# Mamba decays from one product, order of the first chunks and of the square sums, the span of layer 1's GLU, and routing scratch in a weight slot: a four-layer model on one Trainium2 core

## The chip, the core and the metric

The program runs on one NeuronCore of a Trainium2 chip. A time is the device time of one execution in microseconds (us). Before the change three runs gave 3191.99, 3198.89 and 3201.08 us, with a median of 3198.89. One further execution was taken by the hardware profiler, and the times of single instructions below come from it.

## The reference

The input x has 4 sequences of 512 tokens with 256 features, in fp32. Four layers follow, each of the same form:

```
xn = layernorm(x)
x  = x + attention(xn) + ffn(xn)
```

Only the first three matter for the change.

- Layer 0: the attention is a Mamba2 mixer with 32 heads of 64 features and a state of 128. A projection gives a gate, the stream x_s, B, C and a step dt. The state obeys `h = dA_t * h + dt_t * x_t B_t`, with `dA = exp(-dt * exp(A_log))`, and the output is `y_t = h C_t + D x_t`. It is multiplied by silu(gate), scaled by the inverse root of its mean square over all 2048 features, and projected to 256. The feed-forward part is a GLU, `(silu(x Wg) * (x Wu)) Wd`, with 1024 hidden features.
- Layer 1: latent attention with 16 heads of 192 query features and 128 value features, and as feed-forward part a GLU as above plus product-key experts: each token gathers 8 of 512 rows from two tables.
- Layer 2: a mixing of heads within a token, and 8 experts of which each token takes two, plus one shared GLU. Layer 3 is full attention plus experts chosen by a probability mass, and no part of the change touches its work.

## The kernel before, in words

**Tiles.** Tokens are cut into 16 tiles of 128 (`NTILE`), four (`TPB`) per sequence, and 4 sequences (`NB`). Weights are pre-arranged on the host into "units", and `Ctx.unit` (DMA at L53) loads one into a slot "wu" of [128, 3072] fp32. From layer 1 on there are three such slots, in turn: a load waits until the last reader of the unit that had the slot before is through. [...]

**What sets the order.** Every part of a layer is a Python generator that emits instructions and yields an estimate of their TensorE time. `weave` always advances the stream with the smallest ratio of what it has yielded to the total that the call gives for it (with a start offset). A scheduler then orders instructions on each engine by what was emitted and what is ready, except those marked `keep_in_program_order`, and puts in the semaphores. [...] SyncE (SP) issues most DMAs.

**Layer 0** (`mamba_pieces`, woven at L649 with the GLU). The mixer is computed in chunks of 128 tokens for groups of 8 heads: 16 pairs i of sequence and group, four chunks t each.

- `time_steps` computes log dA for all tokens into `dA` [128 tokens, 16 tiles, 32 heads]. Per sequence, four transposes (L326) turn it to [32 heads, 128 tokens], and four products with the triangle `c.le` (L327) give its running sums over a chunk. ScalarE takes the exponential of each (L333), VectorE sets the first column of the one to zero, and two DMAs on SP store them in DRAM as `own` and `since`. L342 makes two more sums over the tokens.
- `decays` (L405) reads `own` back, spread over 128 partitions, as G. `products` (L415) runs a VectorE scan over G, which gives the decay between any two tokens of the chunk. `before` makes the tokens-major x_s (transposes L429, xdt L431), scales x_s by D (L435), and reads `since` as eb.
- `before_gpsimd` multiplies G by C B (L449) and makes xw = xdt times the decay to the chunk's end (L452), both on GpSimd.
- `within` uses them: state times C (L470, then L471 and L472), new state xw times B (L478, L481 to L484), G times xdt (L488), sum and gate (L493, L494), squares (L496).
- `project_out` multiplies y by the output weights into `po` (L510), 256 columns of a "tr" bank. `acc` takes it over (L516; ScalarE's copy for the first group). For the last pair, i = 15, six products with one column of ones (L523) then sum the squares into column 256 of the same bank, and ScalarE copies that column (L527).

Ahead of the loop the first two chunks are prepared by hand, in this order: decays 0 and 1, products 0 and 1, before 0, before_gpsimd 0.

**Layer 1** (`layer1`). Latent attention (16 heads of 4 sequences: scores and softmax L672, L675, L679, L792, their transposes L799 and L803, values and output L935, L941 and L949), the product-key experts (gathers by GpSimd's indirect DMA, L1053) and the GLU (`glu_pieces`: gate and up products L134, activation, down products L212) are woven. The experts' pools and the GLU's pool lie on the right side of SBUF. The stream `room()` starts at 0.915 of the weave: it closes the right side and opens the pools of layer 2 there, loads layer 2's small weights and experts, and runs the routing of the first half of the tokens.

**Layer 2** (`Layer2`). Tokens are taken in two halves. `Half.dispatch` computes router probabilities, ranks and the slots of each token (`router`, L1385, L1447, all small VectorE steps in tiles of the pool "t_route"). `gather` fetches token rows by 23 indirect DMAs (L1482) from `xn_half`, the experts follow (transposes L1500, copies L1505, products L1512 and L1534, results L1539, stores to slots_out L1541), and `combine` gathers the results. The shared GLU's weights are the unit `t_shared`; the units `f_units` are layer 3's attention weights, loaded ahead.

The functions that the diff touches, with their callers:

Of the kernel before, what the change touches and what calls it, by code (L numbers as in the profile page):

```python
# [11 lines left out]
AF = mybir.ActivationFunctionType  # L12
# [3 lines left out]
P = 128  # L16
# [229 lines left out]
def mamba_pieces(c, a, ws, open_pool):  # L246
# [41 lines left out]
    def time_steps():  # L288

        wide_tile = lambda tag: c.tile(pool, wide, tag)  # L290

        pd = c.ps()
        for t in range(NTILE):
            project_tokens(
                c, pd[:, t * 32 : (t + 1) * 32], w_bcd, slice(256, 288),
                slice(t * P, (t + 1) * P),
            )
        z, e = wide_tile("S"), wide_tile("S")
        nc.vector.tensor_add(z, v3(pd, 32), dt_bias[:, None, :].to_broadcast(wide))
        nc.vector.scalar_tensor_tensor(e, z, -1.0, z, ALU.mult, ALU.min)  # L300
        nc.scalar.activation(e, e, AF.Exp)
        expA = c.tile(keep, [P, 32], "expA")
        tc.keep_in_program_order(nc.scalar.activation(expA, a_log, AF.Exp))
        yield 20.0
        s, w, q = wide_tile("xw"), wide_tile("xw"), wide_tile("eb")
        nc.vector.tensor_scalar_add(s, e, 2.0)
        nc.vector.reciprocal(s, s)
        nc.vector.tensor_mul(s, s, e)
        nc.vector.tensor_mul(w, s, s)
        nc.vector.tensor_scalar_mul(q, w, 1.0 / 17.0)  # L310
        yield 20.0
        for k in range(7, 0, -1):
            nc.vector.scalar_tensor_tensor(q, q, 1.0 / (2 * k + 1), w, ALU.add, ALU.mult)
        nc.vector.scalar_tensor_tensor(q, q, 1.0, s, ALU.add, ALU.mult)
        nc.vector.tensor_scalar_max(z, z, 0.0)
        nc.vector.scalar_tensor_tensor(dt, q, 2.0, z, ALU.mult, ALU.add)
        dA = wide_tile("eb")
        nc.vector.scalar_tensor_tensor(
            dA, dt, -1.0, expA[:, None, :].to_broadcast(wide), ALU.mult, ALU.mult
        )  # L320
        yield 38.0
        for b in range(NB):
            pa, pc = c.ps("tr"), c.ps("acc")
            for t in range(TPB):
                cols = slice(t * P, (t + 1) * P)
                nc.tensor.transpose(pa[:32, cols], dA[:, b * TPB + t, :], c.ident)  # L326
                nc.tensor.matmul(  # L327
                    pc[:32, cols], lhsT=dA[:, b * TPB + t, :], rhs=c.le, start=True, stop=True
                )
            tiles = slice(b * TPB, (b + 1) * TPB)  # L330
            for src, out in ((pa, own), (pc, since)):
                row = c.tile(pool, [P, TPB, P], "sq")[:32]
                nc.scalar.activation(row, v3(src[:32, :], P), AF.Exp)  # L333
                if out is own:
                    nc.vector.memset(row[:, :, 0:1], 0.0)
                nc.sync.dma_start(out[tiles].rearrange("t h s -> h t s"), row)
            yield 1.5

        dAf = dA.rearrange("p t h -> p (t h)")
        for tri, out in ((c.gt, after), (c.ones, etot)):  # L340
            pc = c.ps()
            nc.tensor.matmul(pc, lhsT=tri, rhs=dAf, start=True, stop=True)  # L342
            nc.scalar.activation(out.rearrange("p t h -> p (t h)"), pc, AF.Exp)
        yield 2.0
# [100 lines left out]
    def before_gpsimd(i, t):  # L445
        b, g = i // 4, i % 4
        chunk = chunks[i, t]
        G, xdt = chunk[:2]
        nc.gpsimd.tensor_mul(G, G, seqs[b][2][:, t, :][:, None, :].to_broadcast([P, HG, P]))  # L449
        if t < TPB - 1:  # L450
            chunk[2] = xw = c.tile(pool, [P, 512], "xw")
            nc.gpsimd.tensor_mul(  # L452
                v3(xw, HD), v3(xdt, HD), by_head(after[:, b * TPB + t, g * HG : (g + 1) * HG])
            )

    state, sums = {}, []

# [46 lines left out]
    def project_out(i, t, y, sq):  # L504
# [4 lines left out]
        for k in range(4):  # L509
            nc.tensor.matmul(  # L510
                po, lhsT=y[:, k, :], rhs=groups[i][1][:, k, :], start=(k == 0), stop=(k == 3)
            )
        if g == 0:
            nc.scalar.copy(acc[:, t, :], po)
        else:
            nc.vector.tensor_add(acc[:, t, :], po, acc[:, t, :])  # L516
        if i == 15:

            if t == 0:
                sums.append(c.tile(pb, [P, TPB], "sums", bufs=1))  # L520
            parts = [ssq[:, t, k, :] for k in range(2)] + [sq[:, k, :] for k in range(4)]
            for k, part in enumerate(parts):
                nc.tensor.matmul(  # L523
                    bank[:, DM : DM + 1], lhsT=part, rhs=c.ones[:, :1], start=(k == 0),
                    stop=(k == 5),
                )
            nc.scalar.copy(sums[0][:, t : t + 1], bank[:, DM : DM + 1])  # L527
        if g == 3 and t == TPB - 1:
            if i == 15:
                pss = sums[0]  # L530
# [27 lines left out]
    decays(0, 0)  # L558
    decays(0, 1)
    products(0)  # L560
    products(1)
    before(0, 0)
    before_gpsimd(0, 0)
    behind = None
    for i in range(16):
        for t in range(TPB):
# [55 lines left out]
def layer0(c, a, x_in, con):  # L622

    with ExitStack() as stack:
# [12 lines left out]
        def glu_units():  # L637
# [8 lines left out]
        c.parts(2, lambda b: layernorm(c, b, c.xn[b * SEQ : (b + 1) * SEQ, :]))  # L646
        weave(
            c,
            (mamba_pieces(c, a, ws, open_pool), 650.0, 0.0),  # L649
            (glu_units(), 207.0, 0.0),  # L650
        )

# [438 lines left out]
def layer1(c, a, xn, following):  # L1091


    with ExitStack() as stack, ExitStack() as right:
        def pool_of(name, bufs, stack=stack, **kw):
            return stack.enter_context(c.tc.tile_pool(name=name, bufs=bufs, **kw))

        p_keep, p_t, glu = (pool_of(name, 1, right, side="right") for name in ("p_keep", "p_t", "g1"))
        dram = pool_of("p_dram", 1, space=bass.MemoryType.DRAM)
        keep = pool_of("l_keep", 1)  # L1100
        latent = latent_pieces(c, a, keep, lambda: pool_of("l_h", 2))
# [6 lines left out]
        def room():  # L1108
# [6 lines left out]
            c,  # L1115
            (latent, 457.0, 0.0),
            (product_key_pieces(c, a, p_keep, p_t, dram, xn), 237.0, 0.02),
            (glu_units(), 145.0, 0.0),
            (room(), 270.0, 0.915),
            flush=False,  # L1120
        )
# [173 lines left out]
    nc.vector.tensor_mul(s, s, m[:, :, None].to_broadcast(wide))  # L1295


def router(c, pool, wr, bs, p=None, wide=1):

    nc = c.nc
# [15 lines left out]
    yield 2.0  # L1318
    full = [P, n, E, E]
    other, own = p[:, :, None, :].to_broadcast(full), p[:, :, :, None].to_broadcast(full)  # L1320
    before = c.tile(pool, full, "before", bufs=wide)
    tie = c.tile(pool, full, "before" if wide > 1 else "tie", bufs=wide)
    nc.vector.tensor_tensor(before, other, own, ALU.is_gt)
    nc.vector.tensor_tensor(tie, other, own, ALU.is_equal)
    low = v3(c.low, E)[:, None, :, :].to_broadcast(full)
# [10 lines left out]
class Half:  # L1336
# [13 lines left out]

    def dispatch(self):
        c, k, pool, nc = self.c, self.k, self.pool, self.c.nc
        tile = lambda shape, tag, **kw: c.tile(pool, shape, tag, **kw)
        p, rank = tile([P, HT, E8], "p_half"), tile([P, HT, E8], "rank")
        before = yield from router(c, pool, k["router"], [2 * self.hf, 2 * self.hf + 1], p, 4)
        yield 2.0
        nc.vector.tensor_reduce(rank, before[2], AX.X, ALU.add)

# [76 lines left out]
        ats = []  # L1435
        four = [P, 4, P]
        for i in range(2 * HT // 4):
            ats.append(tile(four, "before", bufs=4))
            nc.vector.tensor_tensor(
                ats[i], k["iota"][:, None, :].to_broadcast(four),  # L1440
                part[:, 4 * i : 4 * i + 4][:, :, None].to_broadcast(four), ALU.is_equal,
            )
            yield 1.0
# [238 lines left out]
def program(tc, a, x_in, out):  # L1682
    nc = tc.nc
    with ExitStack() as stack:
# [4 lines left out]
        c.ident, c.le, c.gt, c.ones, c.neg, c.dup = (  # L1689
            con[:, k : k + P] for k in (C_ID, C_LE, C_GT, C_ONE, C_NEG, C_DUP)  # L1690
        )
        c.iota, c.low = con[:, C_IOTA : C_IOTA + 64], con[:, C_LOW : C_LOW + 64]
        eps = c.tile(c.keep, [P, 2], "eps")
        nc.vector.memset(eps[:, 0:1], 1e-5)
# [178 lines left out]
```

## Time and profile before

| what | us |
|---|---|
| median of three runs | 3198.89 |
| the profiled execution | 3204.3 |
| its span, first to last instruction | 3202.2 |
| TensorE (PE) busy | 3099.3 |
| VectorE (DVE) busy | 1820.1 |
| ScalarE (ACT) busy | 1257.2 |
| GpSimd (POOL) busy | 637.9 |

The mean clock granted to TensorE was 0.985 of full speed. On the chain of work that ended last, TensorE holds 85% of the span, VectorE 7%, ScalarE 2% and GpSimd 2%.

Times in the views run from the first instruction. Layer 0 lies at 0 to about 818 us, layer 1 to 1541, layer 2 to about 1760, and layer 3 fills the rest with TensorE busy throughout. An fp32 product shows in the trace as two matmul records, a transpose as one. "Idle before it" and the name behind the arrow say how long an engine stood before an instruction and what released it; "issue" or "remote" there means that the profile names no engine for it.

| DMA from SP | issued at, us |
|---|---|
| t_shared, 768 KB | 1322.96 |
| f_units, first, 1536 KB | 1412.91 |
| f_units, second | 1492.64 |
| f_units, third | 1682.11 |

### The profile page before, as it was taken

The numbers are of one execution on the slowest core, as the hardware profiler recorded it, in microseconds if no ns is written. First come the engines' busy times: TensorE is split into PE (matmuls) and PEld (weight loads), VectorE is DVE, ScalarE is ACT, GpSimd is POOL, SyncE is SP. The second block draws the span as 40 slices with busy tenths as digits, with TensorE's granted clock in tenths as the row PEclk, the third lists the DMA queues.
The fourth block names the chain that finished last, engine by engine and source line by source line (L and its number), as shares of the span: only waits on it lengthen the run. The fifth ranks groups of instructions, "written<-read, shape, count | busy, mean of one in ns | idle before, by whom it ended". The sixth has DMA issues, their size and how long they took to land.

```text
span 3202.2 us, 35743 instructions
## 1 busy us (share of the span) xinstructions
PE 3099.3 (97%) x12534; PEld 1898.2 (59%) x12534; DVE 1820.1 (57%) x4644; ACT 1257.2 (39%) x2918; POOL 637.9 (20%) x509
## 2 busy tenths in 40 slices
PE   8999999999999999998788999999999999999999
PEld 5566666666655555555566566665665655555555
DVE  5777877788587777777354654555545522222222
ACT  4544444453566665666223433333333311111111
POOL 0565555556100233320223000000000000000000
PEclk9999999999999999998799999999999999999999
DMA  3333323332311244443223000000000000000000
GB/s 111 98 109 119 105 83 106 119 99 73 101 38 50 72 117 99 120 113 104 56 64 122 11 1 27 1 27 1 21 1 1 20 20 20 20 20 20 0 0 27
DMA packets 89090, 185.12 MB, mean 58 GB/s; under 512 B 14192, under 2 KB 57216, under 8 KB 84176
## 3 DMA queue, kind: packets, MB, share of 16 engines
q1 hardware_dynamic: 74448, 135.05, 13.0%
q0 software_dynamic: 14176, 47.01, 5.8%
q8 instruction: 99, 1.62, 0.2%
q10 hardware_dynamic: 288, 0.79, 0.1%
q14 instruction: 79, 0.65, 0.1%
HBM read 160.92 MB, written 12.98 MB: 54 GB/s over the span
## 4 chain that ended last, share of the span: by engine, by line
PE 85%; DVE 7%; ACT 2%; POOL 2%; another core or an unknown queue 2%; issue 1%; DMA 1%; SPq 0%; ACTq 0%; DVEq 0%; POOLq 0%
PE mm L134 33%; PE acc L212 8%; PE mm L672 8%; PE mm L142 5%; PE acc L1182 4%; PE acc L688 3%; PE tr L510 2%; PE tr L1174 2%; PE tr L799 2%; PE acc L935 2%; PE acc L949 1%; PE acc L488 1%; PE mm L1512 1%; PE tr L212 1%
## 5 line engine op out<-in xcount | busy, mean ns | idle before, releaser
L134 PE MATMUL mm<-xnT,wu 128*128 128x512 f32 x2128 | 956.5, 597 | 1.1 <-DVE cy L280 0.9
L134 PEld LDWEIGHTS mm<-xnT,wu 128*128 128x128 f32 x2128 | 402.5, 192 | 466.8 <-issue 446.0
L679 ACT ACTIVATE pr<-pr,nm 128x128 f32<-128x128 f32 (+3 forms) x512 | 285.6, 558 | 295.4 <-DVE nm L675 256.4
L202 DVE TENSOR_TENSOR hT<-sg,mm 128x512 f32<-128x512 f32 x176 | 120.6, 685 | 401.3 <-PE mm L134 387.9
L201 ACT ACTIVATE sg<-mm 128x512 f32<-128x512 f32 x176 | 104.6, 594 | 585.6 <-PE mm L134 585.1
L675 DVE CUSTOM_DVE_ANT_0 pr<-mm,late 128x128 f32<-128x128 f32 (+3 forms) x512 | 245.6, 483 | 101.5 <-PE mm L672 89.5
L212 PE MATMUL acc<-wu,hT 128*128 128x256 f32 x1280 | 288.6, 381 | 4.4 <-DVE os L1539 4.4
L212 PEld LDWEIGHTS acc<-wu,hT 128*128 128x128 f32 x1280 | 242.3, 191 | 53.6 <-issue 17.2
L134 PE MATMUL mm<-xnT,w_in 128*128 128x512 f32 x512 | 229.8, 593 | 0.4 <-DVE cy L280 0.4
L1053 POOL DMA_INDIRECT e<-in_p_experts,ids x128 | 129.5, 1012 | 505.4 <-DVE x L152 364.9
L280 DVE SCALAR_TENSOR_TENSOR cy<-mm,ws,cy 128x509 f32<-128x509 f32 (+2 forms) x216 | 160.5, 745 | 49.7 <-ACT cy L276 45.7
L672 PE MATMUL mm<-kf,qf 128*128 128x128 f32 (+3 forms) x512 | 179.7, 450 | 4.1 <-DVE qf L776 2.8
L672 PE MATMUL mm<-k,q 128*128 128x128 f32 (+3 forms) x512 | 178.1, 438 | 1.0 <-DVE q L1147 1.0
L449 POOL TENSOR_TENSOR G<-G,CB 128x1024 f32<-128x1024 f32 x64 | 153.1, 2393 | 101.2 <-DVE G L415 98.0
L435 ACT ACTIVATE xD<-xc,ws 128x128 f32<-128x128 f32 x256 | 83.9, 391 | 197.2 <-POOL y L472 187.5
L134 PEld LDWEIGHTS mm<-xnT,w_in 128*128 128x128 f32 x512 | 96.5, 190 | 104.7 <-issue 95.8
L152 DVE SCALAR_TENSOR_TENSOR x<-acc,cw,x 128x256 f32<-128x256 f32 x128 | 61.9, 484 | 153.6 <-PE acc L212 153.5
L1182 PE MATMUL acc<-PT,V 128*128 128x512 f32 (+3 forms) x512 | 149.1, 433 | 0.0
L415 DVE TENSOR_TENSOR_SCAN G<-G,eye 128x1024 f32<-128x1024 f32 x64 | 146.9, 2296 | 0.0
L1147 DVE TENSOR_SCALAR q<-mm,bias 128x512 f32<-128x512 f32 x64 | 48.0, 751 | 165.1 <-PE mm L134 165.1
L799 PEld LDWEIGHTS tr<-con,pr 128*128 128x128 f32 x640 | 81.3, 143 | 101.1 <-issue 36.6
L799 PE MATMUL tr<-con,pr 128*128 128x128 f32 x640 | 123.5, 284 | 18.3 <-DVE PT L803 6.8
(346 smaller groups left out, 4949.0 us busy)
## 6 DMA issues: line engine op xcount, KB each, us to landing
G<-own SPq DMA_DIRECT2D x64, 512.0 KB
w_in<-in_m_units SPq DMA_DIRECT2D x16, 1024.0 KB
eb<-since SPq DMA_DIRECT2D x96, 128.0 KB
wu<-in_o_units SPq DMA_DIRECT2D x8, 1536.0 KB
wo<-in_m_units SPq DMA_DIRECT2D x16, 512.0 KB
psw<-pes SPq DMA_DIRECT2D x128, 64.0 KB
wu<-in_g_units SPq DMA_DIRECT2D x4, 1536.0 KB
wu<-in_f_units SPq DMA_DIRECT2D x4, 1536.0 KB
```

What stands on the lines that cost most here:

```text
L134: c.nc.tensor.matmul(out, lhsT=w[:, d, cols], rhs=c.xnT[:, d, tokens], start=(d == 0), stop=(d == 1))
L142: c.nc.tensor.matmul(out, lhsT=c.xnT[:, d, tokens], rhs=w[:, d, cols], start=(d == 0), stop=(d == 1))
L212: nc.tensor.matmul(po[:, j, :], lhsT=hT[k][:, (t + j) * P : (t + j + 1) * P], rhs=wd[:, k, :], start=(i == 0), stop=(i == per - 1),)
L280: nc.vector.scalar_tensor_tensor(y[:, j:], src[:, : SEQ - j], conv[:, k, 3 - j : 4 - j], y[:, j:], ALU.mult, ALU.add,)
L415: tc.keep_in_program_order(nc.vector.tensor_tensor_scan(flat, flat, eye.rearrange("p h t -> p (h t)"), 0.0, ALU.mult, ALU.add))
L449: nc.gpsimd.tensor_mul(G, G, seqs[b][2][:, t, :][:, None, :].to_broadcast([P, HG, P]))
L672: nc.tensor.matmul(sc, lhsT=q[:, i * P : n], rhs=k[:, :n], start=True, stop=True)
L675: nc.vector.tensor_tensor_reduce(out=pr, in0=sc, in1=late[:, SEQ - n :], scale=1.0, scalar=-NEG, op0=ALU.add, op1=ALU.min, accum_out=nm,)
L679: nc.scalar.activation(pr, pr, AF.Exp, bias=nm, scale=-1.0, accum_out=total)
L799: nc.tensor.transpose(pt[:, (i - j) * P : (i - j + 1) * P], prs[s][i][:, j * P : (j + 1) * P], c.ident)
L1053: nc.gpsimd.indirect_dma_start(out=e, out_offset=None, in_=a["p_experts"], in_offset=bass.IndirectOffsetOnAxis(ap=ids[:, t, k : k + 1], ax ...
L1182: nc.tensor.matmul(z[:, j * P :], lhsT=head["V"][:, j, h, :], rhs=head["PT"][:, j, j * P :], start=(j == 0), stop=(j == TPB - 1),)
```

## The change

The change has six parts.

1. The decays of one sequence come from one product. The left operand is `dA` of four tiles, 128 tokens by 4 x 32, and the right operand is `c.ident_le`, the identity and the triangle side by side (columns that already lie next to each other in `con`). The result [4 x 32, 256] holds the turned values and the running sums; one exponential, one memset and the same two DMAs follow. The stream's estimates are lowered to match (0.5 for 1.5, and 646 for 650 in all).
2. In the first pair of chunks, `before_gpsimd`'s operations keep program order, and the scan of chunk 1 is emitted after the GpSimd work of chunk 0. On GpSimd the order becomes G 0, xw 0, G 1, xw 1, where it was G 0, G 1, xw 0, xw 1.
3. In `project_out` the sums of squares are emitted directly after the product `po`, ahead of the addition that reads it.
4. The pool of layer 1's GLU moves to the left side, which `room()` doesn't close, and the stream's total is 126 in place of 145, so that its work is spread over more of the weave.
5. In `router` and `dispatch` the tiles before, tie, sel, cum, pick, hit and ats are no longer tiles of the pool, but parts of one weight slot "wu". With this, the turn of the slots changes: each half's dispatch takes one of the three.
6. `c.ident_le` is defined.

```diff
--- before.py
+++ after.py
@@ -320,21 +320,19 @@
         )
         yield 38.0
         for b in range(NB):
-            pa, pc = c.ps("tr"), c.ps("acc")
-            for t in range(TPB):
-                cols = slice(t * P, (t + 1) * P)
-                nc.tensor.transpose(pa[:32, cols], dA[:, b * TPB + t, :], c.ident)
-                nc.tensor.matmul(
-                    pc[:32, cols], lhsT=dA[:, b * TPB + t, :], rhs=c.le, start=True, stop=True
-                )
+
             tiles = slice(b * TPB, (b + 1) * TPB)
-            for src, out in ((pa, own), (pc, since)):
-                row = c.tile(pool, [P, TPB, P], "sq")[:32]
-                nc.scalar.activation(row, v3(src[:32, :], P), AF.Exp)
-                if out is own:
-                    nc.vector.memset(row[:, :, 0:1], 0.0)
-                nc.sync.dma_start(out[tiles].rearrange("t h s -> h t s"), row)
-            yield 1.5
+            pa = c.ps("tr")[:, : 2 * P]
+            nc.tensor.matmul(
+                pa, lhsT=dA[:, tiles, :].rearrange("p t h -> p (t h)"), rhs=c.ident_le,
+                start=True, stop=True,
+            )
+            rows = c.tile(pool, [P, TPB, P], "sq")[:, :2, :]
+            nc.scalar.activation(rows, v3(pa, P), AF.Exp)
+            nc.vector.memset(rows[:, 0, 0:1], 0.0)
+            for k, out in enumerate((own, since)):
+                nc.sync.dma_start(out[tiles].rearrange("t h s -> (t h) s"), rows[:, k, :])
+            yield 0.5
 
         dAf = dA.rearrange("p t h -> p (t h)")
         for tri, out in ((c.gt, after), (c.ones, etot)):
@@ -446,12 +444,16 @@
         b, g = i // 4, i % 4
         chunk = chunks[i, t]
         G, xdt = chunk[:2]
-        nc.gpsimd.tensor_mul(G, G, seqs[b][2][:, t, :][:, None, :].to_broadcast([P, HG, P]))
+
+        keep_order = tc.keep_in_program_order if i == 0 and t < 2 else lambda ins: ins
+        keep_order(
+            nc.gpsimd.tensor_mul(G, G, seqs[b][2][:, t, :][:, None, :].to_broadcast([P, HG, P]))
+        )
         if t < TPB - 1:
             chunk[2] = xw = c.tile(pool, [P, 512], "xw")
-            nc.gpsimd.tensor_mul(
+            keep_order(nc.gpsimd.tensor_mul(
                 v3(xw, HD), v3(xdt, HD), by_head(after[:, b * TPB + t, g * HG : (g + 1) * HG])
-            )
+            ))
 
     state, sums = {}, []
 
@@ -510,10 +512,6 @@
             nc.tensor.matmul(
                 po, lhsT=y[:, k, :], rhs=groups[i][1][:, k, :], start=(k == 0), stop=(k == 3)
             )
-        if g == 0:
-            nc.scalar.copy(acc[:, t, :], po)
-        else:
-            nc.vector.tensor_add(acc[:, t, :], po, acc[:, t, :])
         if i == 15:
 
             if t == 0:
@@ -525,6 +523,10 @@
                     stop=(k == 5),
                 )
             nc.scalar.copy(sums[0][:, t : t + 1], bank[:, DM : DM + 1])
+        if g == 0:
+            nc.scalar.copy(acc[:, t, :], po)
+        else:
+            nc.vector.tensor_add(acc[:, t, :], po, acc[:, t, :])
         if g == 3 and t == TPB - 1:
             if i == 15:
                 pss = sums[0]
@@ -558,9 +560,9 @@
     decays(0, 0)
     decays(0, 1)
     products(0)
-    products(1)
     before(0, 0)
     before_gpsimd(0, 0)
+    products(1)
     behind = None
     for i in range(16):
         for t in range(TPB):
@@ -646,7 +648,7 @@
         c.parts(2, lambda b: layernorm(c, b, c.xn[b * SEQ : (b + 1) * SEQ, :]))
         weave(
             c,
-            (mamba_pieces(c, a, ws, open_pool), 650.0, 0.0),
+            (mamba_pieces(c, a, ws, open_pool), 646.0, 0.0),
             (glu_units(), 207.0, 0.0),
         )
 
@@ -1095,7 +1097,8 @@
         def pool_of(name, bufs, stack=stack, **kw):
             return stack.enter_context(c.tc.tile_pool(name=name, bufs=bufs, **kw))
 
-        p_keep, p_t, glu = (pool_of(name, 1, right, side="right") for name in ("p_keep", "p_t", "g1"))
+        p_keep, p_t = (pool_of(name, 1, right, side="right") for name in ("p_keep", "p_t"))
+        glu = pool_of("g1", 1)
         dram = pool_of("p_dram", 1, space=bass.MemoryType.DRAM)
         keep = pool_of("l_keep", 1)
         latent = latent_pieces(c, a, keep, lambda: pool_of("l_h", 2))
@@ -1115,7 +1118,7 @@
             c,
             (latent, 457.0, 0.0),
             (product_key_pieces(c, a, p_keep, p_t, dram, xn), 237.0, 0.02),
-            (glu_units(), 145.0, 0.0),
+            (glu_units(), 126.0, 0.0),
             (room(), 270.0, 0.915),
             flush=False,
         )
@@ -1295,8 +1298,7 @@
     nc.vector.tensor_mul(s, s, m[:, :, None].to_broadcast(wide))
 
 
-def router(c, pool, wr, bs, p=None, wide=1):
-
+def router(c, pool, wr, bs, p=None, room=None):
 
 
     nc = c.nc
@@ -1318,8 +1320,12 @@
     yield 2.0
     full = [P, n, E, E]
     other, own = p[:, :, None, :].to_broadcast(full), p[:, :, :, None].to_broadcast(full)
-    before = c.tile(pool, full, "before", bufs=wide)
-    tie = c.tile(pool, full, "before" if wide > 1 else "tie", bufs=wide)
+    if room is None:
+        before, tie = c.tile(pool, full, "before"), c.tile(pool, full, "tie")
+    else:
+        before, tie = (
+            v.rearrange("p (t e f) -> p t e f", e=E, f=E) for v in (room[:, :512], room[:, 512:1024])
+        )
     nc.vector.tensor_tensor(before, other, own, ALU.is_gt)
     nc.vector.tensor_tensor(tie, other, own, ALU.is_equal)
     low = v3(c.low, E)[:, None, :, :].to_broadcast(full)
@@ -1350,9 +1356,22 @@
 
     def dispatch(self):
         c, k, pool, nc = self.c, self.k, self.pool, self.c.nc
-        tile = lambda shape, tag, **kw: c.tile(pool, shape, tag, **kw)
+
+        room = c.tile(c.weights, [P, 3072], "wu")
+        ends_at = [2048]
+
+        def tile(shape, tag):
+            if tag not in ("sel", "cum", "pick", "hit"):
+                return c.tile(pool, shape, tag)
+            n = int(np.prod(shape[1:]))
+            flat = room[:, ends_at[0] : ends_at[0] + n]
+            ends_at[0] += n
+            if len(shape) == 3:
+                return v3(flat, shape[2])
+            return flat.rearrange("p (a b c) -> p a b c", b=shape[2], c=shape[3])
+
         p, rank = tile([P, HT, E8], "p_half"), tile([P, HT, E8], "rank")
-        before = yield from router(c, pool, k["router"], [2 * self.hf, 2 * self.hf + 1], p, 4)
+        before = yield from router(c, pool, k["router"], [2 * self.hf, 2 * self.hf + 1], p, room)
         yield 2.0
         nc.vector.tensor_reduce(rank, before[2], AX.X, ALU.add)
 
@@ -1435,7 +1454,7 @@
         ats = []
         four = [P, 4, P]
         for i in range(2 * HT // 4):
-            ats.append(tile(four, "before", bufs=4))
+            ats.append(v3(room[:, i * 512 : (i + 1) * 512], P))
             nc.vector.tensor_tensor(
                 ats[i], k["iota"][:, None, :].to_broadcast(four),
                 part[:, 4 * i : 4 * i + 4][:, :, None].to_broadcast(four), ALU.is_equal,
@@ -1689,6 +1708,7 @@
         c.ident, c.le, c.gt, c.ones, c.neg, c.dup = (
             con[:, k : k + P] for k in (C_ID, C_LE, C_GT, C_ONE, C_NEG, C_DUP)
         )
+        c.ident_le = con[:, C_ID : C_ID + 2 * P]
         c.iota, c.low = con[:, C_IOTA : C_IOTA + 64], con[:, C_LOW : C_LOW + 64]
         eps = c.tile(c.keep, [P, 2], "eps")
         nc.vector.memset(eps[:, 0:1], 1e-5)
```

## The prediction

> **What bounds the kernel now.** First the page: the busy totals, the slices and the chain.
>
> ```profile
> span 3202.2 us, 35743 instructions
> PE 3099.3 (97%) x12534; PEld 1898.2 (59%) x12534; DVE 1820.1 (57%) x4644; ACT 1257.2 (39%) x2918; POOL 637.9 (20%) x509
> ...
> PE   8999999999999999998788999999999999999999
> ...
> PEclk9999999999999999998799999999999999999999
> ```
>
> TensorE is busy for 3099.3 of 3202.2 us. So a change gains in three ways only: less TensorE work, less of the 102.9 us of idle time, or less time at a reduced clock. The slices put both losses at 1440 to 1760 us. The stage windows, read second, split them (columns: window, then length and busy us of PE, PEld, DVE, ACT and POOL, clock, DMA share, GB/s):
>
> ```profile
> 20.00:240.00 220.00, 219.83 (x949) 131.30 (x950) 150.25 (x194) 102.47 (x201) 92.67 (x57) 1.00 0.27 87
> 240.00:790.00 550.00, 541.22 (x2644) 342.05 (x2643) 430.42 (x562) 247.60 (x514) 316.69 (x203) 1.00 0.32 102
> ```
> ```profile
> 1443.20:1453.40 10.20, 7.05 (x16) 3.94 (x17) 6.19 (x23) 5.80 (x17) 3.25 (x3) 0.50 0.44 121
> 1508.10:1514.90 6.80, 6.23 (x17) 4.18 (x18) 4.31 (x22) 4.97 (x14) 0.00 (x0) 0.50 0.16 53
> 1525.10:1531.90 6.80, 6.80 (x19) 4.33 (x19) 1.87 (x12) 1.24 (x3) 0.00 (x0) 0.50 0.00 0
> 1552.40:1579.70 27.30, 5.91 (x14) 3.89 (x13) 3.63 (x8) 3.79 (x5) 13.39 (x15) 0.50 0.36 73
> ```
>
> Layer 0 is bound by TensorE alone: what is cut there at 70 us reaches 240 with nothing to wait for (0.17 us idle), and only 8.8 us are idle from there to 790. The end of layer 1 (1400 to 1541) and layer 2 (to 1760) are not: there the clock stands at half in pieces. Third, the timelines of the two places in layer 0 that are edited (start, length, engine, line, operation, idle before and its releaser):
>
> ```profile
> 73.04 0.27 PE L326 MATMUL tr<-con,eb 128*32 128x128 f32 x1
> 73.24 0.41 PE L327 MATMUL acc<-con,eb 128*32 128x128 f32 x2
> 73.58 0.28 PE L326 MATMUL tr<-con,eb 128*32 128x128 f32 x1
> ```
> ```profile
> 791.65 1.02 PE L478 MATMUL mm<-xw,Btok 128*128 128x512 f32 x2
> ...
> 792.95 2.28 DVE L415 TENSOR_TENSOR_SCAN G<-G,eye 128x1024 f32<-128x1024 f32 x1
> ...
> 795.15 0.40 DVE L516 TENSOR_TENSOR acc<-tr,acc 128x256 f32<-128x256 f32 x1
> ...
> 795.60 0.61 PE L523 MATMUL tr<-con,ssq 128*128 128x1 f32 x4 [2.93 <-DVE acc L516]
> ```
>
> A transpose and its product take 0.55 us of TensorE (73.04 to 73.58). In the second, TensorE stands 2.93 us for an addition of 0.40 us that is queued behind a scan of 2.28 us.
>
> [...]
>
> **The change, part by part.**
>
> *Decays (L322 to L336).* Removed on TensorE: 8 pairs from 67.69 to 72.08 us (4.39), 4 from 73.04 to 75.23 (2.19), and the last 4 apart, 0.44 for the transposes and 0.95 for the products: 7.97 us. Added: 4 products of 128x256, two records each. In the window 1100 to 1200, 32 records of this shape (L212) take 7.44 us, 0.233 each, so 8 take 1.86. Gain 7.97 - 1.86 = 6.1; if the new product also shows its 0.19 us weight load each time, 5.4, the lower end. ScalarE does 4 exponentials of [128, 256] for 8 of [32, 512]; it is busy 9 of the 20 us there and bounds nothing. The DMAs stay two per sequence at the same place of SP's queue, ahead of the `eb` and G loads, which wait for them as before; the G load issued at about 78 us serves a scan at 93, so 10 us of slack.
>
> *First chunks (L449, L452, L558 to L563).* No work changes. GpSimd now multiplies G 0, xw 0, G 1, xw 1, where it did G 0, G 1 (6.51 us from 95.52), xw 0 at 101.99. TensorE came for xw 0 at 102.9 and waited 0.17 us. By the decays it comes 6 us earlier, about 96.9, and would wait some 6 us; with the new order xw 0 is ready after one G product and the 1.04 us of xw, some 3.3 us sooner and moved up with the scans. Gain 0.2 by itself; it keeps the 6.1. Behind the waiting product on TensorE stand the next chunk's products and the GLU filler; if xw 0 is late, up to 3 us of the 6.1 are lost.
>
> *Sums (L516, L523).* Placed ahead of the reading addition, six one-column products per tile wait only for squares made earlier. The 2.93 us wait goes; the half-clock piece of 798.1 to 801.5, which costs 1.7, may go too. The addition now waits for the sums (0.61 + 1.03 us on TensorE), and VectorE, nearly full at 792 to 801, is late next: its chain to the next output product doesn't shorten. Ends 1 and 4.6; I take 3.
>
> *Layer 1's GLU.* The work is the same, its last sequence comes later. A sequence of one unit is 15.0 us of L134 and 7.4 of L212 (one in each 100 us from 1100 to 1400). Before, the last ended at 1436, where 82% of the L672 score products are placed; after, at 95%. By the order on TensorE 11 to 19 us of GLU move beyond that point. Lost there, 1436 to 1541: about 10.5 us idle, and 23.8 us at half clock, so 11.9. Of this, 4.25 idle (1442 to 1447) falls on every engine at once beside a run of gathers, with no engine named as releaser: no filler helps, nor the half clock that follows it. The 3.9 idle at 1504 to 1509 and the two later half-clock pieces (6.8) come when the GLU is over again. Left: 2.6 idle, some 3 of clock at 1446 to 1453, and what the 1508 piece gives. Against it, 13% thinner filler at 900 to 1400, where 13 us are idle: 1 to 2 more. Also, VectorE gets 7 us of GLU steps where it is 60 to 75% busy. Ends -3 and +14; I take +5.
>
> *Routing scratch in a weight slot.* No operation changes. But slots rotate: by the order on SP, read against times before, the `t_shared` load moves from 1323 to about 1493, still ahead of its use at 1527; `f_units` 0 and 1 (1.5 MB each) move from 1413 and 1493 to about 1546 and 1626, beside the two runs of 23 gathers. On SP the first stands ahead of the first slots_out stores (1597), the second between two stores, behind a routing product that TensorE has already passed. The gathers are issued every 1.25 us and move 92 GB/s at 1541 to 1580; windows elsewhere reach 186 GB/s. With 1.5 MB more in 29 us, 92 + 54 = 146 GB/s, still below; I take 0.5, ends 0 and 10 for both.
>
> Sum: 6.1 + 0.2 + 3 + 5 - 0.5 = 13.8 us. The profiled execution took 3204.3 us (span 3202.2, 2.1 around it), so 3190.5 of its kind; it lay 5.4 above the median 3198.89. Against the median, 3185.1.
>
> **Rivals.**
>
> *Late GLU gives nothing.* For it: the stalls beside gathers stop all engines. Against: 2.6 us of plain waits lie in reach. Then 13.8 - 5 = 8.8 gained; with -1 for thin filler and clock, 3191.
>
> *Late GLU closes the whole tail.* If those stalls are waits that other work can fill: 10.5 + 11.9 = 22.4, less 2 for thin filler and less what lies after 95%, 14 to 16. Then 13.8 + 10 = 24, 3175.
>
> *Slower: loads beside the gathers of layer 2.* TensorE stands for 20.67 us (L1512, releaser ACT xsT) until 1575, when the last gather has landed; a like gap comes at 1638. If a load of 1.5 MB holds the gathers back for its whole time at their rate, 1.57/0.092 = 17 us, twice, 34: 3199 - 14 + 34 = 3219. From 7 us each the gain is gone; from 12 each the kernel is measurably slower. For it: that gap is the longest on TensorE, and its cause is open. Against: DMA share 0.36 there.
>
> *The decays' saving is swallowed* (the chain own, G, scan, G times CB, xw arrives no sooner, or the product is no cheaper): 3191, one with the first rival in its number.
>
> **How the numbers follow.** Forecast 0.45 (3178 to 3192), late GLU or decays without gain 0.28, whole tail 0.14, slower by the loads 0.10, other 0.03. About 0.3% is what a measurement of this kernel can tell from no change: 9.6 us, so below 3189.3 and above 3208.5. Faster: 0.37 of the forecast, 0.11 of the first rival, 0.14 of the third case, 0.62. Slower: 0.08 of the loads and 0.02 of other, 0.10. Same: 0.28. The range leaves out the best of the whole tail and most of the loads: 3168 to 3201.
>
> **What would show it.** In the profile of after: 8 records of the new product at about 0.23 us, and the first L134 after them 6 us sooner; xw's product with no wait over 1 us near 97 us; no wait of L523 on L516; L212 records up to about 1510 and fewer half-clock pieces before 1541; the first gap of layer 2 no longer than 20.7 us. I am wrong if the gathers' gap grows by over 7 us, if PE idle at 900 to 1400 rises by over 5, or if TensorE waits for xw.

## The result and the profile after

| | before | changed |
|---|---|---|
| median of six runs, us | 3197.89 | 3175.51 |
| lowest and highest | 3191.99 to 3204.61 | 3166.72 to 3178.26 |

The ratio is 0.993, with a 95% interval of 0.9915 to 0.9945: 22.4 us faster (18 to 27). The forecast was 13.8. The page of the changed kernel, the same lines as before:

```profile
span 3171.8 us, 35654 instructions
...
PE 3078.8 (97%) x12494; PEld 1883.7 (59%) x12494; DVE 1819.0 (57%) x4644; ACT 1251.1 (39%) x2912; POOL 638.6 (20%) x509
...
PE   8999999999999999999788999999999999999999
...
PEclk9999999999999999999899999999999999999999
```

TensorE's idle time fell from 102.9 to 93.0 us and its busy time by 20.5. Busy time includes what half clock adds: in the trace of before, four L134 records take 3.55 us to the next line's start at 1527.1, where the granted clock is 0.50, and 1.80 at 29.9, where it is 1.00. So half of the time at half clock is counted as lost below, an estimate from these two. The two profiled spans differ by 30.4 us, 8 more than the medians. Of this, 5.6 us lie ahead of every edit: an L134 pair takes 2.06 us until about 26 us in the one execution and until 16 in the other, and 1.10 from there on. So the stages are compared from a fixed record of layer 0's GLU (at 37.0 and 31.3 us) to the first score product of layer 1 (at 878.4 and 849.5): 841.5 us before, 818.2 after. By then the changed kernel is 23.3 us ahead, and from there to the end it gains 1.5 more. But some 3.4 of the 23.3 are not gained, only moved: 8 records of L134, 0.43 us each, stand ahead of that score product before and behind it in the changed kernel, as in all traces with the late GLU. So about 20 us lie in layer 0 and the head of layer 1, and about 5 behind.

The decays, on TensorE's timeline of the changed kernel (mm, tr and acc are tags of the kernel's PSUM pool, with 4, 2 and 2 tiles):

```profile
62.07 1.03 PE L326 MATMUL tr<-con,eb 128*128 128x256 f32 x4
62.94 1.88 PE L340 MATMUL mm<-eb,con 128*128 128x512 f32 x4
64.65 1.03 PE L326 MATMUL tr<-con,eb 128*128 128x256 f32 x4
65.52 2.74 PE L134 MATMUL mm<-xnT,w_in 128*128 128x512 f32 x6
```

From each start to the next line's start four records take 0.87 us (62.07 to 62.94, 64.65 to 65.52): 1.74 us in all, for 7.97 before. The sums, on the timeline at the end of layer 0:

```profile
771.62 1.89 PE L512 MATMUL tr<-wo,y 128*128 128x256 f32 x8
...
773.35 0.50 PE L521 MATMUL tr<-con,ssq 128*128 128x1 f32 x4
...
777.40 0.41 DVE L529 TENSOR_TENSOR acc<-tr,acc 128x256 f32<-128x256 f32 x1
```

They follow their product with no idle time, and the addition comes 4 us behind them, with nobody waiting. Last, layer 1 in two windows, before and after:

```profile
880.00:1408.00 528.00, 513.25 (x2218) 294.30 (x2217) 408.83 (x1412) 334.84 (x897) 106.57 (x105) 0.99 0.32 83
1408.00:1541.00 133.00, 119.47 (x547) 73.00 (x546) 90.09 (x318) 85.65 (x209) 16.04 (x17) 0.91 0.33 105
```
```profile
880.00:1380.00 500.00, 482.13 (x2083) 271.98 (x2083) 383.35 (x1319) 316.83 (x849) 109.20 (x110) 1.00 0.33 83
1380.00:1512.00 132.00, 124.15 (x571) 75.90 (x568) 90.30 (x312) 83.97 (x206) 12.28 (x13) 0.95 0.28 82
```

In the last window TensorE idles 7.9 us for 13.5, and its mean clock is 0.95 for 0.91 (6.6 us lost for 12, if the missing share of the clock is taken as time). In the window ahead of it, it idles 17.9 us for 14.8: the filler is thinner.

### The profile page after: what moved, and what is told of

Read it like the earlier page. It is cut to its first block, busy times and chain, and to the rows that moved or that the text cites. A ratio compares the mean times of both kernels' runs of the same rounds, so it can differ in the third digit from the quotient of the medians.

```text
span 3171.8 us, 35654 instructions
## 1 busy us (share of the span) xinstructions
PE 3078.8 (97%) x12494; PEld 1883.7 (59%) x12494; DVE 1819.0 (57%) x4644; ACT 1251.1 (39%) x2912; POOL 638.6 (20%) x509
## 4 chain that ended last, share of the span: by engine, by line
PE 85%; DVE 6%; ACT 2%; another core or an unknown queue 2%; issue 2%; POOL 1%; DMA 1%; SPq 0%; ACTq 0%; DVEq 0%; POOLq 0%
PE mm L134 33%; PE acc L212 8%; PE mm L674 7%; PE mm L142 5%; PE acc L1185 4%; PE acc L690 3%; PE tr L512 3%; PE tr L1177 2%; PE tr L801 2%; PE tr L212 2%; PE acc L937 2%; PE acc L490 2%; PE mm L1531 1%; PE acc L951 1%
## 5 line engine op out<-in xcount | busy, mean ns | idle before, releaser
L134 PE MATMUL mm<-xnT,wu 128*128 128x512 f32 x2128 | 953.0, 596 | 0.0
L134 PEld LDWEIGHTS mm<-xnT,wu 128*128 128x128 f32 x2128 | 401.2, 191 | 463.6 <-issue 442.4
L134 PE MATMUL mm<-xnT,w_in 128*128 128x512 f32 x512 | 229.2, 593 | 0.6 <-DVE cy L280 0.6
L280 DVE SCALAR_TENSOR_TENSOR cy<-mm,ws,cy 128x509 f32<-128x509 f32 (+2 forms) x216 | 160.2, 744 | 50.3 <-ACT cy L276 46.4
L134 PEld LDWEIGHTS mm<-xnT,w_in 128*128 128x128 f32 x512 | 96.5, 190 | 104.3 <-issue 94.0
L152 DVE SCALAR_TENSOR_TENSOR x<-acc,cw,x 128x256 f32<-128x256 f32 x128 | 61.9, 484 | 153.7 <-PE acc L212 153.6
```

The source lines that it names most:

```text
L134: c.nc.tensor.matmul(out, lhsT=w[:, d, cols], rhs=c.xnT[:, d, tokens], start=(d == 0), stop=(d == 1))
L280: nc.vector.scalar_tensor_tensor(y[:, j:], src[:, : SEQ - j], conv[:, k, 3 - j : 4 - j], y[:, j:], ALU.mult, ALU.add,)
```

## The experiments

Twelve runs, each beside runs of the kernel before on the same chip; two of them repeat a kernel on another chip. Three chips came up: the first four ran on one (before: 3193.9 us), the next four on a second (3132.5), the last four on a third (3131.4). So ratios are compared, and traces by stretches; a gain in us is the ratio applied to the median of before. The stretch is that from the fixed record to the first score product; "sums" is TensorE's wait ahead of L523 (L521), "L142" its longest wait at the head of layer 1, "half clock" the time between 740 and 880 us with a granted clock of 0.50.

| kernel | stretch, us | sums | L142 | half clock | ratio to before, 95% |
|---|---|---|---|---|---|
| before (profiled) | 841.5 | 2.9 | 3.0 | 6.8 | |
| scratch alone | 842.8 | 2.9 | 3.0 | 10.2 | 1.0006 (0.9999 to 1.0013) |
| decays alone | 838.7 | 3.7 | 5.7 | 13.7 | 0.9994 (0.9986 to 1.0002) |
| decays alone, old pace | 838.9 | 2.9 | 5.8 | 13.7 | 0.9994 (0.9986 to 1.0003) |
| sums alone | 837.7 | 0 | 3.8 | 6.8 | 0.9986 (0.9977 to 0.9995) |
| changed, decays undone | 834.5 | 0 | 3.6 | 6.8 | 0.9964 (0.9951 to 0.9978) |
| changed, sums undone | 834.8 | 3.7 | 5.5 | 13.7 | 0.9965 (0.9951 to 0.998) |
| layer 0 alone | 825.3 | 0 | 2.0 | 3.4 | 0.9936 (0.9922 to 0.9949) |
| the same, third chip | 824.9 | 0 | 2.0 | 3.4 | 0.9934 (0.9922 to 0.9946) |
| changed, first comparison | 818.2 | 0 | 1.7 | 0 | 0.993 (0.9915 to 0.9945) |
| changed, GLU early | 823.6 | 0 | 2.0 | 0 | 0.9936 (0.9923 to 0.9949) |
| changed, old pace | 821.7 | 0 | 1.5 | 0 | 0.9942 (0.9928 to 0.9956) |
| changed, chunks in old order | 820.9 | 0 | 1.7 | 0 | 0.9946 (0.9934 to 0.9959) |
| changed, third chip | 819.5 | 0 | 1.7 | 0 | 0.9909 (0.9894 to 0.9924) |

In all rows named "changed" but GLU early, the 8 records of L134 lie behind the end of the stretch, which is some 3.4 us shorter for that alone. The two traces of the changed kernel itself are 1.3 us apart (818.2 and 819.5).

After the first comparison the theory was: the edits add, each where it is made (decays 6.7 us at 60 to 80, 5 by better mixing behind them, sums 5, layer 1 some 4). The rivals: the better mixing is a difference between two executions, the decays' gain is swallowed, and layer 1 gives all or nothing.

**Decays alone.** The edit, on the kernel before:

```diff
-            pa, pc = c.ps("tr"), c.ps("acc")
...
+            pa = c.ps("tr")[:, : 2 * P]
+            nc.tensor.matmul(
+                pa, lhsT=dA[:, tiles, :].rearrange("p t h -> p (t h)"), rhs=c.ident_le,
...
-            yield 1.5
+            yield 0.5
...
-            (mamba_pieces(c, a, ws, open_pool), 650.0, 0.0),
+            (mamba_pieces(c, a, ws, open_pool), 646.0, 0.0),
```

> The kernel before with the decays' new product and its lower pace alone; the first chunks keep their old order. If the decays' gain stays and the better mixing of layer 0 at 240 to 560 us is its doing too: 6.7 + 5.6 = 12 us faster, less what TensorE waits for the first xw (L450 of this kernel, before 0.17 us): up to 6. If that wait swallows the gain: 0 to 3 us faster, with a gap of about 6 us on TensorE at 97 us. If the better mixing was only a difference between two executions: 6 us faster at most, and idle time of 8 to 9 us at 240 to 790 as before.

Measured: 0.9994, 2 us (-1 to 4), and neither expectation. No wait of 6 us arose at the first xw; the gain stood until 740 us (10.6, the 5.4 of the start taken off) and was given back afterwards: 6.8 at the last sum, 2.8 at the first score product. Its timeline:

```profile
78.76 2.32 DVE L280 SCALAR_TENSOR_TENSOR cy<-mm,ws,cy 128x511 f32<-128x511 f32 x3 [1.77 <-ACT cy L276]
80.99 4.46 DVE L413 TENSOR_TENSOR_SCAN G<-G,eye 128x1024 f32<-128x1024 f32 x2
...
89.90 1.04 POOL L450 TENSOR_TENSOR xw<-xdt,after 128x512 f32<-128x512 f32 x1
...
90.99 1.13 PE L476 MATMUL mm<-xw,Btok 128*128 128x512 f32 x2 [0.17 <-POOL xw L450]
...
780.17 0.96 PE L521 MATMUL tr<-con,ssq 128*128 128x1 f32 x4 [3.70 <-DVE acc L514]
...
805.45 0.90 SPq L1049 DMA_DIRECT2D tok<-xn_tokens  x2
...
805.62 2.77 ACTq L806 DMA_DIRECT2D psw<-in_l_rope  x1
...
808.42 1.28 ACT L90 ACT_TABLE_LOAD   x1 [3.29 <-DMA tok<-xn_tokens]
...
815.00 2.08 PE L142 MATMUL mm<-wu,xnT 128*128 128x256 f32 x4 [5.66 <-DVE sg L166]
```

The same two steps of VectorE in the kernel before:

```profile
90.85 2.32 DVE L280 SCALAR_TENSOR_TENSOR cy<-mm,ws,cy 128x511 f32<-128x511 f32 x3 [0.45 <-ACT cy L276]
93.08 4.46 DVE L415 TENSOR_TENSOR_SCAN G<-G,eye 128x1024 f32<-128x1024 f32 x2
```

In both, the scan starts where VectorE's convolution steps (L280) end, and these follow products of TensorE. So the chain of the first chunk, scan, G and xw, came forward together with TensorE, by 12.1 us, of which 5.4 are the start. At the end of layer 0 the wait ahead of the sums is longer than before, and the one at L142 nearly twice as long.

**Sums alone.** The two hunks of `project_out`, on the kernel before:

```diff
+        if g == 0:
+            nc.scalar.copy(acc[:, t, :], po)
+        else:
+            nc.vector.tensor_add(acc[:, t, :], po, acc[:, t, :])
         if g == 3 and t == TPB - 1:
```

> The kernel before with the sums of squares directly after their product, and nothing else. If the wait on the addition was the cost: 3 us faster, 5 if the half-clock piece at 798 us goes with it, and no gap ahead of the sums. If VectorE's chain takes its place: within 1 us of before, with the idle time now ahead of L212 or the next output product.

Measured: 0.9986, 4.5 us (2 to 7). The wait was the cost; VectorE's chain didn't take its place, though the wait at L142 grew from 3.0 to 3.8 us.

**GLU early.** The changed kernel with

```diff
-        glu = pool_of("g1", 1)
+        p_keep, p_t, glu = (pool_of(name, 1, right, side="right") for name in ("p_keep", "p_t", "g1"))
...
-            (glu_units(), 126.0, 0.0),
+            (glu_units(), 145.0, 0.0),
```

> The changed kernel with layer 1's GLU back on the right side and at its old pace of 145, all else kept. If the late GLU gives 5 us: 17 us faster than before, in place of 22. If it gives nothing: 22. If it carries the whole tail: 8 to 12. In the trace the idle time of TensorE in the last 140 us of layer 1 should go back from 6.5 to about 14 us, with 20 to 24 us at half clock, whichever holds for the total.

Measured: 0.9936, 20.4 us. Against 22.4 of the changed kernel (another set of runs) the late GLU is worth 2 us, inside both intervals: the whole-tail rival is out, a gain of 5 isn't excluded. The trace went back nearly as expected: in the last 140 us before layer 2's gathers TensorE idles 12.0 us with 20.5 at half clock, for 7.9 and 13.7 in the changed kernel. Why so little of this reaches the total is shown below.

**Chunks in their old order.** The changed kernel without `keep_order`, and with

```diff
     products(0)
+    products(1)
     before(0, 0)
     before_gpsimd(0, 0)
-    products(1)
```

> The changed kernel with the old order of the first two chunks. If the mended order protects the decays' gain: TensorE waits 3 to 6 us for the first xw near 91 us, and the kernel is 16 to 19 us faster than before. If the wait is hidden by filler that the scheduler puts there: 22 us faster as the changed kernel, with no gap over 1 us.

Measured: 0.9946, 17 us; but TensorE waited only 0.17 us for the first xw. The total fits the first expectation, the place doesn't: the stretch is 2.7 us longer, or 1.4 by the changed kernel's other trace, with no gap to go with it. The medians, 3174.5 for 3175.5 us, show no loss. What this edit is worth in the total is not resolved.

**Layer 0 alone.** The kernel before with the hunks of decays, chunks, sums and pace.

> The kernel before with the three edits of layer 0 (decays, first chunks, sums); layer 1's GLU and the routing scratch stay. If the whole gain is made in layer 0, where the decays' saving only holds once the sums no longer wait: 19 to 22 us faster, as the changed kernel. If the edits of layer 1 carry the rest: 8 us, the sum of decays alone (2.4) and sums alone (5.8).

Measured: 0.9936, 20 us. Most of the gain is made in layer 0, and together the edits give far more than 2 and 4.5.

**Decays undone, scratch alone, sums undone.** The hunks of the decays and their pace, and those of the sums, each taken back from the changed kernel; and the routing scratch put alone into the kernel before:

```diff
-            ats.append(tile(four, "before", bufs=4))
+            ats.append(v3(room[:, i * 512 : (i + 1) * 512], P))
```

> The changed kernel with the old decays (pairs of transpose and product, old pace), all else kept. If the decays give 6.7 us at 60 to 80 us and the better mixing behind them 5: 10 to 12 us faster than before. If they give nothing, as alone: 20 us. In the trace, TensorE idles 8 to 9 us at 240 to 790 us if the mixing is their doing, 4 to 5 us if not.

Measured: 0.9964, 11 us; idle time at 240 to 750 us 9.1 us, so the better mixing comes with the decays' edit, of which the pace is a part.

> The kernel before with the routing scratch in a weight slot, and nothing else: the slots turn otherwise. By the prediction 0 to 1 us slower, 0 to 10 if the weight loads beside layer 2's gathers hold these back. If the sums and the decays are not all, and the loads that leave the gathers of layer 1 free give the rest: 5 to 10 us faster.

Measured: 1.0006, 2 us slower (0 to 4), hardly told from no change. In its trace, on the second chip, TensorE waits 1 us at most at the gathers, so the rival that loads hold them back is judged by the first comparison.

> The changed kernel with the sums behind the addition again, all else kept. If the sums add 5 us whatever the decays do: 16 us faster than before. If the decays' saving holds only with them: 3 to 10 us faster, with the wait of 3 to 4 us ahead of the sums and pieces at half clock behind it.

Measured: 0.9965, 11 us faster than before, near the second expectation. The wait is 3.7 us, and 13.7 us pass at half clock, as with the decays alone.

**The pace.** The two estimates alone, in the decays alone and in the changed kernel:

```diff
-            yield 0.5
+            yield 1.5
...
-            (mamba_pieces(c, a, ws, open_pool), 646.0, 0.0),
+            (mamba_pieces(c, a, ws, open_pool), 650.0, 0.0),
```

> The kernel before with the new product, but the old pace (yields of 1.5, total of 650), so that the mixing with the GLU stays as it was. If the loss at the end of layer 0 in the decays alone comes from the new mixing: 6 us faster than before, with a wait ahead of the sums of about 3 us as before. If it comes of arriving earlier, whatever the mixing: 2 us faster, with 12 to 13 us of idle time at 750 to 880. The idle time at 240 to 750 us falls from 8.8 to below 5 if the product itself does that, and stays if the pace does.

> The changed kernel with the decays' old pace (yields of 1.5, total of 650). If the pace is worth the 4 us of idle time at 240 to 750: 4 us slower than the changed kernel beside it. If the product itself is: no difference.

> The changed kernel itself, as the reference for the three beside it: 20 to 22 us faster than before. In its trace the TensorE idle time at 240 to 750 us should be 4 to 5 us and that at 750 to 880 5 to 7, if these belong to the kernel and not to the execution.

The decays alone came out at 0.9994 with either pace, so the new mixing is not what loses the gain. The changed kernel gave 0.9909, 28 us and more than expected, with the old pace 0.9942: 3104.9 against 3111.5 us, 6.6 apart (2 to 15 by resampling the runs). The windows 240 to 740 and 740 to 880 of the old pace, then of the changed kernel beside it:

```profile
240.00:740.00 500.00, 492.01 (x2369) 309.18 (x2368) 387.95 (x513) 228.83 (x473) 286.83 (x184) 1.00 0.33 105
740.00:880.00 140.00, 136.08 (x684) 89.98 (x683) 105.33 (x271) 70.74 (x202) 44.75 (x45) 1.00 0.30 95
```
```profile
240.00:740.00 500.00, 495.56 (x2398) 312.32 (x2397) 391.62 (x518) 230.17 (x477) 291.01 (x186) 1.00 0.33 105
740.00:880.00 140.00, 134.70 (x671) 88.78 (x670) 104.36 (x277) 72.65 (x207) 42.00 (x43) 1.00 0.30 94
```

Idle time in the first window is 8.0 us with the old pace and 4.4 with the new; in all kernels with the new pace, at 240 to 750 us, it lies at 4 to 5, in all with the old at 8 to 9. So 3.6 us come from the estimates, not from the product. In the second window 1.4 of them are taken back (3.9 us with the old pace, 5.3 with the new), and the stretch is 2.2 us shorter. The traces show no more than that of the 6.6.

**Layer 0 alone, beside the changed kernel.**

> The kernel before with the three edits of layer 0 alone, on the chip of the changed kernel. If the edits of layer 1 give nothing: the same as the changed kernel within 2 us. By the prediction: 4.5 us slower than it (5 for the GLU, less 0.5 for the loads).

Measured: 0.9934 beside 0.9909; medians 3109.1 and 3104.9, 4.2 us apart, by resampling the runs 1 to 12. The edits of layer 1 give about what was forecast on this chip. By its ratio no version was faster than the changed kernel.

## Why the prediction was right, and where it was not

The direction, the stated range and the price of the decays in place held. The sum was short by 8.6 us, mainly because the decays and the sums were costed apart and depend on each other. That the range held is in part luck: the median of 3175.5 us lies below the forecast's own band (3178 to 3192) and on the number of the rival in which the late GLU closes the whole tail (3175), and GLU early, 20 us faster than before without the late GLU, rules that mechanism out.

- **Decays, 6.1.** Right: 7.97 - 1.74 = 6.2 in place, and the shift of 5.6 us ahead of the edit is 12.7 at the first chunk, 7.1 more. A step that failed is what came with it: the pace, "the stream's estimates", got no price, and is worth 3.6 us of idle time at 240 to 740, of which 2.2 are left at the end of the stretch. The rival that the saving is swallowed came true for the decays alone, but at the end of layer 0, not at xw.
- **First chunks.** The step "TensorE comes 6 us earlier and would wait some 6 us" failed: the wait was 0.17 us with the old order too. It took the scan to stand still while TensorE moves; but the scan follows VectorE's steps on TensorE's own products. In place the new order is worth 0.4 us: the first chunk comes 7.1 us earlier with it and 6.7 without, the start taken off.
- **Sums, 3.** Alone 4.5 (2 to 7), the upper end. With the decays there, 11 to 18 (0.9965 without them; 0.993 and 0.9909 with, on other chips). The step that failed took the end of layer 0 as it stood before, where one wait of 2.9 us was to go. That the sums waited for the addition is measured (2.93 us before, 0 in the sums alone); why they did, when it reads other columns than they write, was not shown.
- **Late GLU, 5.** The plan held: layer 1's last down product ends 37 us ahead of layer 2's first gather in the changed kernel, 126 in GLU early. Here are two windows of GLU early, as long as those of the changed kernel shown above, and the tail of layer 0 alone and of the changed kernel on the third chip:

```profile
884.00:1384.00 500.00, 490.24 (x2127) 281.18 (x2127) 387.20 (x1326) 316.66 (x848) 105.49 (x105) 1.00 0.35 81
1384.00:1516.00 132.00, 120.86 (x553) 72.61 (x552) 91.75 (x322) 84.31 (x213) 17.20 (x18) 0.92 0.32 86
```
```profile
1365.00:1497.00 132.00, 122.14 (x568) 74.91 (x566) 95.24 (x335) 91.15 (x226) 17.20 (x18) 0.94 0.35 108
```
```profile
1361.00:1493.00 132.00, 128.66 (x589) 76.86 (x588) 94.77 (x325) 87.06 (x216) 16.42 (x17) 0.96 0.31 88
```

In the tail, idle time and clock, reckoned as above, cost 21.7 us in GLU early (11.1 + 10.6) and 14.5 in the changed kernel; on the third chip 17.8 and 8.6. So the tail gives 7 to 9 us. The step that failed is the price of the thinner filler ahead of it, "1 to 2 more": there TensorE idles 17.9 us for 9.8, and 8.9 for 6.2 on the third chip. By the prediction's own sign, PE idle at 900 to 1400 up by over 5, it was wrong on this: 12.6 us before, 18.9 after. What is left is 2 us on the first chip and, with the scratch, 4.2 by medians on the third; there the tail's gain outweighs the cost. (The tail of before was also misread: it idles 11.3 us at 1436 to 1541, not 10.5, and 3.2 at 1504 to 1509, not 3.9.)

- **Scratch, -0.5.** The loads went to 1464, 1519 and 1598 us, beside the gathers, which is where the prediction put them, less the 27 to 29 us by which all came forward. That a load beside the gathers can hold them back was the author's assumption; layer 2's gap was 19.8 us for 20.7, so the slower rival is out.

**Where the two edits of layer 0 meet.** Each alone gives 2 and 4.5 us; both, with the chunks' order, give 20. With the chunks in their old order the changed kernel still shows none of the losses below, so that edit isn't needed for them to go. The windows 740 to 880 of before, of the decays alone and of the changed kernel show it:

```profile
740.00:880.00 140.00, 131.88 (x650) 87.92 (x648) 95.84 (x199) 64.41 (x177) 50.92 (x49) 0.98 0.28 88
```
```profile
740.00:880.00 140.00, 127.36 (x598) 85.71 (x599) 90.92 (x214) 62.23 (x176) 43.13 (x44) 0.95 0.31 94
```
```profile
740.00:880.00 140.00, 134.86 (x672) 88.87 (x671) 104.63 (x278) 72.84 (x207) 42.03 (x43) 1.00 0.29 92
```

Idle time and half of the time at half clock make 8.1 + 3.4 = 11.5 us before, 12.6 + 6.8 = 19.4 with the decays alone, 5.1 with all. So of the decays' 10.6 us nearly all, 8, are given back here. The sums saved 2.5 of the 11.5 in the trace of the sums alone (5.6 + 3.4 left); in the changed kernel they save some 15 (13.6 + 6.8 = 20.4 with the sums undone). Three things make up the loss of the decays alone. The wait ahead of the sums is 3.7 us for 2.9 with the new pace. Each of the two long gaps is followed by 6.8 us at half clock, for 3.4 before. And the gap at L142 is 5.7 us for 3.0, with ScalarE held in its own DMA issue ahead of it for 2.77 us. That issue takes 0.41 in the changed kernel, whose timeline has

```profile
793.71 0.41 ACTq L810 DMA_DIRECT2D psw<-in_l_rope  x1
793.82 0.90 SPq L1053 DMA_DIRECT2D tok<-xn_tokens  x2
...
800.76 1.13 PE L142 MATMUL mm<-wu,xnT 128*128 128x256 f32 x4 [1.75 <-DVE PT L865]
```

Here ScalarE issues 0.11 us ahead of SP's two loads, there 0.17 behind them. Behind the issue on ScalarE stand a table load (1.28 us), the inverse root (L90), and with it VectorE's L152, the layernorm and L166, which TensorE waits for. In the five kernels with only one of the two edits the issue comes second and takes 2.2 to 2.9 us; in before, scratch alone and the seven runs with both, it comes first and takes 0.41. From ScalarE's last copy of the sums to the product at L142, 9.3 to 10.2 us pass in the five, and 7.1 to 7.7 in all the others. That the order of the two issues is the cause is read from the traces; moving that DMA was not tried, and why the order turns is open.

The time at half clock doesn't follow the length of a gap alone in these traces. Before and scratch alone have the same two gaps, 2.9 and 3.0 us, and 6.8 against 10.2 us at half clock; a gap of 2.0 us is followed by 3.4 in layer 0 alone and by none in GLU early. These are different chips, and what decides is open; one piece of 3.4 us more or less, by the estimate above a loss of 1.7, is not to be read as an effect of an edit. The pieces with a clock of 0.50 last 3.4, 6.8, 10.2 and 27.3 us in the trace of before, and 3.4, 6.8 and 27.3 in the changed kernel's up to 1552 us. In before, one begins at 798.1, 2.5 us after the gap of 2.9 us has ended. That closing a gap also takes away the piece behind it was the prediction's assumption: it didn't in the sums alone, where the gap ahead of the sums is gone and 6.8 us at half clock remain.

What stays open: the first chunks' worth in the total, and the rest of the interaction. The stretch accounts for 16 to 17 of the 20 us of layer 0 alone.

## What to carry to other kernels

Cost an edit at the next place where the bound engine has to stop, too: time gained far upstream is kept only if the stage's end isn't held by another chain, and two edits that each look small there can be worth several times their sum. The estimates that a weave works with are an edit of their own; give them a price, or change them in a run of their own. And when work arrives earlier, ask whether what it waits for follows the bound engine too, and so comes earlier as well. Filler that is moved to one place is missing at another: price both ends.

## What the runs showed of the hardware that was not expected

**One chip of three was 2% slower, and mostly at the gathers.** The code of layers 1 and 2 is the same in the decays alone (first chip) and in the decays alone at the old pace (third). Their windows 1530 to 1560, in that order:

```profile
1530.00:1560.00 30.00, 9.67 (x56) 6.87 (x54) 2.47 (x8) 2.68 (x5) 19.92 (x21) 0.63 0.49 114
```
```profile
1530.00:1560.00 30.00, 30.00 (x139) 23.05 (x139) 17.85 (x39) 11.30 (x18) 16.51 (x17) 0.94 0.43 92
```

On the first chip every compute engine but GpSimd stands through most of the gathers, with "remote" as the releaser (VectorE 25.1 us, ScalarE 26.2), and TensorE waits 20.9 us for xsT; on the third TensorE is busy throughout, its longest wait for xsT is 1.0 us, and "remote" is not among the waits of these engines there. GpSimd issues the gathers every 1.25 us on both. Before's medians differ by 62 us; in these two traces 59 lie between the first score product of layer 1 and that of layer 3. So a gap like the longest one in the profile that the prediction worked from was there on one chip and not on another with the same code; its cause is open.

**One DMA issue took ScalarE 2.2 to 2.9 us in five of the fourteen traces, and 0.41 in the other nine.** It is a load of 256 KB. The 0.41 us came 0.11 us ahead of two loads on SP, in before and in the changed kernel; the 2.8 us of the decays alone and the 2.2 of the sums alone came 0.17 us behind them.

**The start.** TensorE runs its first products at about half speed until 14 to 16 us in nine of the fourteen traces and until 26 to 28 in five (L134 pairs of 2.06 us, then 1.10), which is some 5.5 us between two profiles of the same code ahead of every edit. The clock column says 1.00 there, but the trace holds no clock record before that moment (26.7 us before, 15.5 after); only the durations show it.
